# Three changes to the last stretch of an attention-and-involution kernel: own buffers for VectorE's products, weight copies made at once, additions queued by when their products should be ready

## The chip, the core and the metric

The kernel runs on one core of one Trainium2 chip. The metric is the device time of one execution in microseconds (us). The median of 3 runs before the change is 2592.14 us (2591.94 to 2592.26).

A core has several engines that run their own instruction queues in order: TensorE (PE in the profile; its weight loads are PEld), VectorE (DVE), ScalarE (ACT), GpSimd (POOL) and SyncE (SP), which here issues nearly all transfers. They meet by semaphores.

## The reference, cut to what matters

All data is float32. The input is 4 images of 512 channels and 64 x 64 pixels. Two layers follow each other.

```python
# layer 0: attention over all 4096 pixels of an image, with a residual
q = wq @ xf + bq;  k = wk @ xf + bk;  v = wv @ xf + bv        # 128 channels each
attn = softmax(q^T k)                                        # 4096 x 4096 per image
x = wo @ (v @ attn^T) + bo + x                               # back to 512 channels

# layer 1: involution, a 7x7 filter whose weights depend on the pixel
out = relu(s1 * (W1 @ x) + b1)                               # 128 channels, 8 groups of 16
w = Ws @ relu(sr * (Wr @ out) + br) + bs                     # 49 taps x 8 groups per pixel
out[g, c, pixel] = sum over 49 taps of w[g, tap, pixel] * out[g, c, pixel + tap]
x = s3 * (W3 @ out) + b3 + x
```

## The kernel before, in words

For each image `b` the function `keys_values` computes keys and values, and `attention` walks over blocks of queries: score matmuls (`pss`), an exponential on ACT (`pt`), and a matmul with the values (`po`). A finished block goes to `finish_block`, a generator that divides by the sums, adds the residual, computes the first product of layer 1 (`p1`), writes its pixels to DRAM (`pix`) and makes `red`, from which the tap weights come. The last image's last block is cut into two of 256 pixels, named `7_0` and `7_256` below.

The involution is done in units. A unit is 4 rows of 64 pixels, so 16 units to an image; `b, u` names it. Pixels lie on the partitions and channels along a row. The function `weights` makes the tap weights of a unit with two matmuls into a PSUM tile `pw`. Image rows come from `pix` by DMA into `ring`, a buffer of 12 rows. The taps of a unit are grouped into instructions: one product (line 417) multiplies ring rows by tap weights, for one column offset and 1 to 4 row offsets at once, 256, 512, 768 or 1024 columns. The first products of a unit go straight into its accumulator `acc`. Every other product goes into a buffer `prod` and is then added.

While attention runs, DVE makes all products and POOL adds them (line 445). After the last `attention` call the list `tail` is filled, and only then does this stretch differ, which is the part that the change touches:

- `share` (line 185) chooses for each product who makes it and who adds it: DVE then PE, DVE then POOL, or POOL then PE. It keeps in `spent` the time that it expects each engine to have spent, and takes the choice that keeps the longest of them shortest. The prices are the constants of line 77.
- [...] when POOL first makes a product of a unit, `copied` (line 310) has ACT copy the two halves of `pw` into an SBUF tile `w`, which is taken from the pool of the x tiles.
- All products, whoever makes them, take turns in the 4 buffers of the pool `prods`.
- When PE adds, `turned_add` (line 253) issues one 128 x 128 transposing matmul for each 128 columns, accumulating in a PSUM tile `pa`. These are queued at once behind each product. A unit's `acc` is added last, by `add_sums` in `turn_unit`. The finished `pa` is copied to `accT`, and `close_chunk` multiplies it (`py`), adds the result to x and writes x out.

The loop over `finishing`, `closing` and `taps` at the end of `fast_path` issues one step of each in turn. A recording layer then orders the instructions on each engine; in the last stretch it may move products. Two engines that read the same PSUM tile are made to wait for each other by that layer, in the order in which the code names them.

In the last stretch three units are left, 13, 14 and 15 of image 3, besides the end of unit 12 on POOL and the end of block `7_256`.

Of the kernel before, what the change touches and what calls it, by code (L numbers as in the profile page):

```python
# [15 lines left out]
P = 128  # L16
CT = C // P
CH = 512
# [55 lines left out]
HOP_US = 0.8  # L74
STEP_US = 1.0
POOL_LAG = 4.0, 7.5
DVE_COL, POOL_COL, PE_ADD = (0.064, 1.042e-3), (0.13, 2.19e-3), 0.115
PIECE = 3
TB = 32
WARM = 8  # L80
# [7 lines left out]
def fast_path(  # L88
# [22 lines left out]
    def pool(name, bufs, **kw):  # L111
        return ctx.enter_context(tc.tile_pool(name=name, bufs=bufs, **kw))

    const = pool("const", 1)
    xpool = pool("x", 6)
    kvpool = pool("kv", 1)
    ptpool = pool("pt", 5)
    redpool = pool("red", 3)
    work1 = pool("work1", 1)
    work2 = pool("work2", 2)  # L120
    prods = pool("prods", 4)
    scratch = pool("scratch", 1, space=bass.MemoryType.DRAM)
    ps = pool("ps", 2, space=bass.MemoryType.PSUM)
    ps1 = pool("ps1", 1, space=bass.MemoryType.PSUM)
# [2 lines left out]
    ps_s = scorepool.enter_context(  # L127
        tc.tile_pool(name="ps_s", bufs=2, space=bass.MemoryType.PSUM, reuse_waits="tile")
    )
    wpools, early = [ps1], {}  # L130

    wt = const.tile([P, O_WR], F32, name="wt")
    vec = const.tile([P, NVEC], F32, name="vec")
# [29 lines left out]
    due, seen = 0.0, 0.0  # L163
    free = {"dve": 0.0, "pool": 0.0, "dma": 0.0}
    tail = []
    spent = {}
    reds, sums_c = {}, {}
    written = {}
    landing = {}
# [14 lines left out]

    def share(cols, adds, direct):

        by = {
            "dve": DVE_COL[0] + DVE_COL[1] * cols,
            "pool": POOL_COL[0] + POOL_COL[1] * cols,
            "pe": PE_ADD * cols / P,  # L190
        }
        ways = [("dve", "pe"), ("dve", "pool"), ("pool", "pe")]
        if direct:
            ways = ways[:1]

        def after(way):
            us = dict(spent)
            us[way[0]] += by[way[0]]
            if adds:
                us[way[1]] += by[way[1]]  # L200
            return us

        way = min(ways, key=lambda w: sorted(after(w).values(), reverse=True))
        spent.update(after(way))
        return way
# [102 lines left out]


    def copied(b, u, pw):  # L310
        w = xpool.tile([P, CT, CH], F32, tag="x", name=f"w_{b}_{u}")
        for t in range(NT):
            nc.scalar.copy(w[:, t, : NTAP * G], pw[:, t, : NTAP * G])
        return w

    def weights(b, u):
# [31 lines left out]
    def involution():  # L348
        nonlocal low, due
        while True:  # L350
            while not units:
                yield "none"
            b, u = units.pop(0)
            acc = work2.tile([P, NT, 4, P], F32, tag="acc", name=f"acc_{b}_{u}")
            yield from until(free["dve"] + 0.3)
            pw = early.pop((b, u), None) or weights(b, u)
            begin = pe + 0.5
            pw_copy = None
            pa, ops = None, []
            base = b * STEP + u * UR  # L360
            for dy0, n in DYS:

                at = (base + dy0) % RING
                whole = at + n + NT < RING + 1
                pieces = [(dy0, n)] if whole else [(dy0, 2), (dy0 + 2, n - 2)]
                ops += [((0, 1), x, dy, k) for x in range(K) for dy, k in pieces]
            ending = (b, u) == (B - 1, NU - 1)
            if ending:

                ops = [op for op in ops if op[2] < DYS[1][0]]  # L370
                for x in range(K):
                    ops += [((0, 1), x, 4, 1), ((0,), x, 5, 2)]
            for o, (tiles, x, dy, n) in enumerate(ops):
                if o and dy >= DYS[1][0] > ops[o - 1][2]:
                    low = base + UR
                    pump()
                    if tail and units:
                        early[units[0]] = weights(*units[0])
                rows = [(base + dy + t * 2) % RING for t in range(NT)]
                while base + dy + n + 2 * tiles[-1] > load:  # L380
                    yield "wait"
                landed = max(landing[base + dy + 2 * t + i] for t in tiles for i in range(n))
                while not tail and (
                    pe < max(begin, landed)
                    or free["dve"] > pe + (4.5 if b == B - 1 else 3.5)
                    or free["pool"] > pe + lag
                ):
                    yield "wait"
                first = x == 0 and dy < DYS[1][0]
                maker = adder = None  # L390
                if tail:
                    maker, adder = share(
                        n * len(tiles) * P, not first, first or ending and o >= len(ops) - 6
                    )
                cost = n * len(tiles) / NT
                free["pool"] = max(free["pool"], takes("dve", DVE_TAPS[0] + DVE_TAPS[1] * cost))
                takes("pool", POOL_TAPS[0] + POOL_TAPS[1] * cost)
                due -= cost
                d0 = dy - DYS[dy >= DYS[1][0]][0]
                prod, p0 = acc, d0  # L400
                if not first:
                    prod, p0 = prods.tile(
                        [P, NT, 4, P], F32, tag="prod", name=f"prod_{b}_{u}_{o}"
                    ), 0
                nt = len(tiles)
                col = (x * K + dy) * G
                lines = ring[:, rows[0] : rows[0] + n, x, :]
                image = bass.AP(
                    tensor=lines.tensor, offset=lines.offset,
                    ap=[lines.ap[0], [(rows[1] - rows[0]) * K * P, nt], [K * P, n], [1, P]],  # L410
                )
                maps = pw
                if maker == "pool":
                    if pw_copy is None:
                        pw_copy = copied(b, u, pw)
                    maps = pw_copy
                product = (nc.gpsimd if maker == "pool" else nc.vector).tensor_tensor(  # L417
                    prod[:, :nt, p0 : p0 + n, :].rearrange("p t d (g c) -> p t d g c", g=G),
                    image.rearrange("p t d (g c) -> p t d g c", g=G),
                    maps[:, :nt, col : col + n * G].unsqueeze(3)  # L420
                    .broadcast_to([P, nt, n * G, GC])
                    .rearrange("p t (d g) c -> p t d g c", d=n),
                    ALU.mult,
                )
                if not tail:
                    tc.keep_in_program_order(product)
                if first:
                    pass
                elif adder == "pe":

                    begun = pa is not None
                    if not begun:
                        pa = ps1.tile([P, NT, P], F32, tag=("po", "acc")[u % 2], name=f"pa_{b}_{u}")
                    closes = ending and o == len(ops) - 1
                    if closes:
                        add_sums(pa, acc, False)
                    for t in tiles:
                        for d in range(n):
                            turned_add(
                                pa[:, t, :], prod[:, t, d, :],  # L440
                                not begun and t == d == 0,
                                closes and t == tiles[-1] and d == n - 1,
                            )
                else:
                    nc.gpsimd.tensor_tensor(  # L445
                        acc[:, :nt, d0 : d0 + n, :], acc[:, :nt, d0 : d0 + n, :],
                        prod[:, :nt, :n, :], ALU.add,
                    )
                yield
            low = max(low, (b + 1) * STEP if u == NU - 1 else base + UR)  # L450
            pump()
            if pa is None:
                for n in (2, 1):
                    nc.gpsimd.tensor_tensor(  # L454
                        acc[:, :, :n, :], acc[:, :, :n, :], acc[:, :, n : 2 * n, :], ALU.add
                    )
            closing.append(turn_unit(b, u, acc, pa, takes("pool", POOL_OP * 1.5)))


    def add_sums(pa, acc, closes):  # L460
        for t in range(NT):
            for d in range(4):
                spend("pe", PE_ADD)
                turned_add(
                    pa[:, t, :], acc[:, t, d, :], False, closes and t == NT - 1 and d == 3
                )


    def turn_unit(b, u, acc, pa, done):
        c, k = divmod(u, 2)  # L470
        yield from until(done + 2.0)
        for _ in range(7 if tail else 0):
            yield
        if pa is None and b < B - 1:

            blocks = work2.tile([P, NT * P], F32, tag="turned", name=f"turned_{b}_{u}")
# [316 lines left out]
    for b in range(B):  # L793
# [26 lines left out]
            )  # L820
        attention(b, *kv)
    tail.append(True)
    spent.update(pe=0.0, **{e: max(free[e] - pe, 0.0) for e in ("dve", "pool")})
    scorepool.close()
    wpools.insert(0, pool("ps_w", 1, space=bass.MemoryType.PSUM, reuse_waits="tile"))
# [405 lines left out]
```

## Time and profile before

| | before |
|---|---|
| median of 3 runs | 2592.14 us |
| the profiled execution's own time | 2591.92 us |
| its span | 2590.0 us |
| granted TensorE clock, mean | 0.999 |
| last `po` matmul ends, from the start of the span | about 2532.1 us |
| first `pa` add of the last stretch | 2536.24 us |
| last `x<-py` on DVE starts (two in 0.92 us) | 2584.14 us |

A span is the time from the first to the last instruction. In a row of the timeline the first number is the start in us, the second the length, then engine, line, operation, tiles (`out<-in`), shapes and how many instructions the row merges; in brackets stands the idle time before it and what ended it. A row of the waits names who waited for whom, the total in us, how often, and the longest. A wait for several semaphores is put down to the one that came last. A 512-column float32 matmul shows as two records, a transposing add as one.

### The profile page before, as it was taken

To read this page: it belongs to the slowest core of one execution; us is meant where nothing else is said; L and a number is where in the kernel's file an instruction comes from. 1 tells how busy PE (TensorE), PEld (TensorE's weight loads), DVE (VectorE), ACT (ScalarE), POOL (GpSimd) and SP (SyncE) were. 2 spreads that over 40 slices of the span, in tenths; PEclk is the share of its full clock that TensorE was granted. 3 is DMA by queue.
4 is the path that set the end of the run, shared out by engine and by line. 5 is a ranking of instruction groups with operands and counts; after the bars stand their busy time and mean duration, and the time that the engine had idled before them with its cause. 6 is when DMAs were issued, how large, how long until landed. Compare 5 with 4: busy or idle time off the path is not lost.

```text
span 2590.0 us, 24394 instructions
## 1 busy us (share of the span) xinstructions
PE 2575.1 (99%) x7398; PEld 1232.7 (48%) x7398; DVE 1861.7 (72%) x2668; ACT 838.0 (32%) x1385; POOL 1814.8 (70%) x1198
## 2 busy tenths in 40 slices
PE   9999999999999999999999999999999999999998
PEld 7444444445544444444554444444464444444476
DVE  0347778887585787888666667887856678787887
ACT  1333333332233333333223333333323333333331
POOL 0006788877881778888786368887878477787985
PEclk9999999999999999999999999999999999999999
DMA  6033233445615343234651434434363431332343
GB/s 238 1 74 63 57 78 82 98 101 150 153 54 114 63 101 76 65 82 93 169 149 41 108 69 98 100 69 102 79 182 101 116 94 48 79 77 61 77 108 88
DMA packets 208473, 243.36 MB, mean 94 GB/s; under 512 B 109576, under 2 KB 128464, under 8 KB 208208
## 3 DMA queue, kind: packets, MB, share of 16 engines
q1 hardware_dynamic: 207904, 241.39, 38.6%
q8 instruction: 59, 0.97, 0.2%
q14 instruction: 78, 0.64, 0.1%
q10 hardware_dynamic: 432, 0.36, 0.1%
HBM read 192.65 MB, written 49.06 MB: 93 GB/s over the span
## 4 chain that ended last, share of the span: by engine, by line
PE 91%; POOL 4%; DVE 3%; issue 1%; DVEq 0%; POOLq 0%; ACT 0%; ACTq 0%
PE pss L251 32%; PE po L251 31%; PE pv L251 4%; PE pk L251 4%; PE pq L251 4%; PE py L251 4%; PE pwo L251 4%; PE p L251 4%; POOL acc L445 3%; PE pw L251 2%; DVE prod L417 1%; DVE pacc L783 1%; PE pa L255 1%; PE pr L251 1%; POOL acc L454 0%
## 5 line engine op out<-in xcount | busy, mean ns | idle before, releaser
L445 POOL TENSOR_TENSOR acc<-acc,prod 128x768 f32<-128x768 f32 (+3 forms) x1044 | 1670.7, 1618 | 740.2 <-DVE prod L417 696.8
L251 PE MATMUL pss<-q,k 128*128 128x512 f32 (+1 forms) x2112 | 1055.7, 584 | 0.0
L251 PE MATMUL po<-pt,v 128*128 128x512 f32 (+1 forms) x2112 | 1047.2, 580 | 0.0
L752 ACT ACTIVATE pt<-pss 128x512 f32<-128x512 f32 x1024 | 611.0, 597 | 1242.7 <-PE pss L251 1171.4
L417 DVE TENSOR_TENSOR prod<-ring,pw 128x768 f32<-128x768 f32 (+3 forms) x1081 | 875.3, 844 | 51.2 <-POOL acc L445 45.0
L783 DVE TENSOR_TENSOR pacc<-pacc,pt 128x512 f32<-128x512 f32 x958 | 665.5, 695 | 237.5 <-ACT pt L752 209.4
L251 PEld LDWEIGHTS po<-pt,v 128*128 128x128 f32 x2112 | 398.8, 190 | 480.9 <-issue 460.4
L251 PEld LDWEIGHTS pss<-q,k 128*128 128x128 f32 x2112 | 391.5, 190 | 466.8 <-issue 462.0
L478 DVE STREAM_TRANSPOSE turned<-acc 128x256 f32<-128x256 f32 x48 | 21.4, 445 | 217.8 <-POOL acc L454 217.8
L251 PE MATMUL py<-accT,wt 128*128 128x512 f32 (+1 forms) x264 | 132.3, 584 | 4.1 <-DVE x L534 3.3
L251 PE MATMUL pwo<-on,wt 128*128 128x512 f32 (+1 forms) x264 | 128.5, 579 | 0.0
L454 POOL TENSOR_TENSOR acc<-acc 128x512 f32<-128x512 f32 x122 | 121.4, 995 | 9.6
L251 PEld LDWEIGHTS pv<-wt,x 128*128 128x128 f32 x1024 | 119.6, 192 | 15.3 <-issue 15.3
L534 DVE SCALAR_TENSOR_TENSOR x<-py,vec,x 128x512 f32<-128x512 f32 (+1 forms) x132 | 95.8, 727 | 36.9 <-PE py L251 36.7
L251 PE MATMUL pv<-wt,x 128*128 128x128 f32 x1024 | 120.2, 275 | 0.0
L251 PE MATMUL p<-x,wt 128*128 128x512 f32 (+1 forms) x264 | 119.3, 580 | 0.0
L251 PE MATMUL pk<-x,wt 128*128 128x512 f32 x256 | 117.5, 598 | 0.0
L663 ACT ACTIVATE x<-x,vec 128x512 f32<-128x512 f32 (+1 forms) x132 | 93.0, 707 | 72.3 <-PE p L251 58.2
L251 PE MATMUL pq<-x,wt 128*128 128x512 f32 (+1 forms) x264 | 115.3, 579 | 0.0
L636 DVE SCALAR_TENSOR_TENSOR x<-pwo,bo,x 128x512 f32<-128x512 f32 (+1 forms) x132 | 95.3, 728 | 21.8 <-PE pwo L251 20.4
L417 DVE TENSOR_TENSOR acc<-ring,pw 128x1024 f32<-128x1024 f32 (+1 forms) x84 | 78.7, 956 | 16.4 <-PE pw L251 15.6
L251 PEld LDWEIGHTS pq<-x,wt 128*128 128x128 f32 x264 | 50.1, 190 | 59.7 <-issue 56.4
(71 smaller groups left out, 731.4 us busy)
## 6 DMA issues: line engine op xcount, KB each, us to landing
x<-x_dram SPq DMA_DIRECT2D x55, 1024.0 KB, 5.7
ring<-pix SPq DMA_DIRECT2D x74, 448.0 KB, 6.7
ring<-pix SPq DMA_DIRECT2D x24, 1344.0 KB, 9.7
out_dram<-x SPq DMA_DIRECT2D x31, 1024.0 KB, 4.5
ring<-pix SPq DMA_DIRECT2D x24, 896.0 KB, 10.6
ring<-pix SPq DMA_DIRECT2D x30, 672.0 KB, 10.8
ring<-pix SPq DMA_DIRECT2D x6, 2240.0 KB, 19.5
pix<-o1t SPq DMA_DIRECT2D x192, 32.0 KB, 1.7
```

Source lines behind the costliest of these rows:

```text
L251: return nc.tensor.matmul(o, lhsT=lhsT, rhs=rhs, start=start, stop=stop)
L255: nc.tensor.matmul(o, lhsT=lhsT, rhs=ident, start=start, stop=stop, is_transpose=True)
L417: product = (nc.gpsimd if maker == "pool" else nc.vector).tensor_tensor(prod[:, :nt, p0 : p0 + n, :].rearrange("p t d (g c) -> p t d g c", ...
L445: nc.gpsimd.tensor_tensor(acc[:, :nt, d0 : d0 + n, :], acc[:, :nt, d0 : d0 + n, :], prod[:, :nt, :n, :], ALU.add,)
L454: nc.gpsimd.tensor_tensor(acc[:, :, :n, :], acc[:, :, :n, :], acc[:, :, n : 2 * n, :], ALU.add)
L478: nc.vector.transpose(blocks.rearrange("p (t k q) -> p t k q", t=NT, q=TB), acc[:, :, 0, :].rearrange("p t (k q) -> p t k q", q=TB),)
L534: nc.vector.scalar_tensor_tensor(xt[:, t, :], py, v1(V_S3 + t), xt[:, t, :], ALU.mult, ALU.add)
L636: nc.vector.scalar_tensor_tensor(xt[:, t, :], pw, bo[:, t : t + 1], xt[:, t, :], ALU.add, ALU.add)
L663: nc.scalar.activation(xt[:, t, :], xt[:, t, :], AF.Identity, bias=v1(V_B3 + t))
L752: nc.scalar.activation(pt, pss, AF.Exp)
L783: nc.vector.tensor_tensor(paccs[k], paccs[k], pt, ALU.add)
```

## The change

Nothing is changed before the last stretch but the place of pools in SBUF.

- The pool of keys and values gets a stack of its own, opened after the others, and is closed when the last attention is issued. Two new pools take its room: `tail_w`, 3 tiles for weight copies, and `tail`, 5 buffers for the products that DVE makes. POOL's products stay in the 4 buffers of `prods`.
- The copy of a unit's weights is issued when its first product is, or, for the next unit, right behind its `weights`, whether POOL turns out to need it or not.
- POOL's price for a product is told apart from that for an addition.
- PE's additions are not queued at once. They go into a list with the time at which the maker should be done; `drain` queues, in order of these times, all that lie behind the time DVE has reached by the plan, and the rest of a unit when the unit is closed.

The diff, cut to its core:

```diff
-DVE_COL, POOL_COL, PE_ADD = (0.064, 1.042e-3), (0.13, 2.19e-3), 0.115
+DVE_COL, POOL_COL, POOL_ADD, PE_ADD = (0.064, 1.042e-3), (0.19, 1.66e-3), (0.13, 2.19e-3), 0.115
...
-    kvpool = pool("kv", 1)
...
     prods = pool("prods", 4)
+    kvstack = ExitStack()
+    kvpool = kvstack.enter_context(tc.tile_pool(name="kv", bufs=1, reuse_waits="tile"))
+    tailpools = []
...
     def share(cols, adds, direct):
-        by = {
+        made = {
             "dve": DVE_COL[0] + DVE_COL[1] * cols,
             "pool": POOL_COL[0] + POOL_COL[1] * cols,
-            "pe": PE_ADD * cols / P,
         }
+        added = {"pool": POOL_ADD[0] + POOL_ADD[1] * cols, "pe": PE_ADD * cols / P}
...
     def copied(b, u, pw):
-        w = xpool.tile([P, CT, CH], F32, tag="x", name=f"w_{b}_{u}")
+        w = tailpools[0].tile([P, NT, NTAP * G], F32, tag="w", name=f"w_{b}_{u}")
...
                     if tail and units:
                         early[units[0]] = weights(*units[0])
+                        copies[units[0]] = copied(*units[0], early[units[0]])
...
                 if tail:
+                    if pw_copy is None:
+                        pw_copy = copies.pop((b, u), None) or copied(b, u, pw)
                     maker, adder = share(
...
                 if not first:
-                    prod, p0 = prods.tile(
+                    home = tailpools[1] if maker == "dve" else prods
+                    prod, p0 = home.tile(
...
                 elif adder == "pe":
-                    begun = pa is not None
...
-                    for t in tiles:
-                        for d in range(n):
-                            turned_add(
...
+                    closes = ending and o == len(ops) - 1
                     if closes:
-                        add_sums(pa, acc, False)
...
+                        drain(sums)
+                        add_sums(sums["pa"], acc, False)
+                    adds.append((spent[maker], o + 100 * u, sums, prod, tiles, n, closes))
...
+                if tail:
+                    drain()
                 yield
...
+    def drain(unit=None):
+        due = sorted(a for a in adds if a[2] is unit or a[0] <= spent["dve"] or a[6])
+        for a in due:
+            adds.remove(a)
+            _, _, sums, prod, tiles, n, closes = a
...
+            for t in tiles:
+                for d in range(n):
+                    turned_add(
+                        sums["pa"][:, t, :], prod[:, t, d, :],
...
     def turn_unit(b, u, acc, sums, done):
...
         for _ in range(7 if tail else 0):
             yield
+        drain(sums)
+        pa = sums.get("pa")
...
     tail.append(True)
+    kvstack.close()
+    tailpools += [pool("tail_w", 3, reuse_waits="tile"), pool("tail", 5, reuse_waits="tile")]
```

## The prediction

> **What bounds the kernel now.** I read the page first: engine totals, then the chain that ended last.
>
> ```profile
> PE 2575.1 (99%) x7398; PEld 1232.7 (48%) x7398; DVE 1861.7 (72%) x2668; ACT 838.0 (32%) x1385; POOL 1814.8 (70%) x1198
> ...
> PE 91%; POOL 4%; DVE 3%; issue 1%; DVEq 0%; POOLq 0%; ACT 0%; ACTq 0%
> ```
>
> TensorE is busy throughout and carries the chain. The orders of the two built programs are the same on all five queues until the attention of the last image ends (last `po` at 2532.1 us), so I keep that time. What can move is the 57.9 us behind it, where units 13, 14 and 15 of image 3 are made. I read this by stretches, then the engines' timelines, then the waits.
>
> ```profile
> 2532.90:2545.00 12.10, 11.49 (x78) 9.11 (x77) 10.59 (x19) 4.01 (x9) 6.90 (x6) 1.00 0.41 125
> 2545.00:2550.80 5.80, 5.43 (x46) 4.72 (x44) 5.09 (x10) 0.96 (x3) 3.07 (x5) 1.00 1.05 211
> ...
> 2556.70:2568.00 11.30, 9.68 (x60) 6.54 (x58) 10.13 (x12) 0.87 (x2) 7.59 (x6) 1.00 0.11 44
> ...
> 2575.00:2582.00 7.00, 6.14 (x39) 4.47 (x37) 4.40 (x12) 0.67 (x2) 1.58 (x3) 1.00 0.23 77
> ```
>
> The columns are length, then busy time (and instructions) of PE, PEld, DVE, ACT, POOL, then granted clock (1.00, so no throttling). PE looks full even here, but a `pa` record (0.272 us) is longer than its pace, so short waits hide in it:
>
> ```profile
> 2536.24 0.49 PE L255 MATMUL pa<-ident,prod 128*128 128x128 f32 x3
> ...
> 2542.57 2.13 PE L255 MATMUL pa<-ident,prod 128*128 128x128 f32 x18
> ...
> 2545.90 4.67 PE L255 MATMUL pa<-ident,prod 128*128 128x128 f32 x36
> ...
> 2581.22 0.38 PE L255 MATMUL pa<-ident,prod 128*128 128x128 f32 x2
> 2582.12 2.41 PE L251 MATMUL py<-accT,wt 128*128 128x256 f32 x8 [0.52 <-ACT accT L517]
> ```
>
> Eighteen adds in 2.13 us is (2.13 - 0.272)/17 = 0.109 each; 56 in 6.33 us elsewhere gives 0.110; the 36 in 4.67 us take 0.126, so 0.6 us there is hidden waiting. I use 0.110. From the first `pa` (2536.24) to the end of the last (2581.60) are 45.4 us. PE's own work in it: 270 adds x 0.110 = 29.7; four 512-column `py` x 0.865 (0.86 to 0.87 in the chain) = 3.5; four 256-column `py` and four `pwo` x 0.44 (the chain has two `pwo` in 0.89) = 3.5; `pw_15` 0.9; `pn` 0.1; the last `p`, `pp` and `pr` 1.1. Sum 38.8, so PE waits **6.6 us**. From the end of the last `pa` to the end of the span are 8.4 us, which the change does not touch. The waits say for what:
>
> ```profile
> ACT w L313 <- DVE acc L417: 10.7, 2, 7.0
> POOL prod L417 <- PE pa L255: 7.0, 11, 1.5
> ...
> POOL prod L417 <- ACT w L313: 4.7, 2, 4.2
> DVE prod L417 <- PE pa L255: 4.5, 8, 0.9
> POOL acc L445 <- DVE prod L417: 3.9, 3, 2.7
> ```
>
> It is a ring: both makers wait for one of four shared buffers, which PE frees; PE waits for a product of the slower maker; POOL waits for a weight copy that itself stands behind a DVE product.
>
> **The change, part by part.**
>
> *Room.* The DVE's product pool and the pool of weight copies now lie where keys and values lay. Their last readers are the last `pss` (2528.6) and `po` (2532.1), before any tail product in either order: 0. The other pools shift in address. No row shows a cost of an address; the runs' spread bounds it to 0.3 us either way, I take 0.
>
> *Buffers.* DVE gets five of its own, POOL keeps the four. In the new order most DVE products wait only for PE's adds of five DVE products ago. This is what ends DVE's 4.5 us and most of POOL's 7.0.
>
> *Weight copies.* Six ACT copies (0.49 each, 0.88 a pair) move ahead; they issue no DMA, and the wait for an x buffer's old output transfer goes. `pw_13` ends at 2532.9, so `w_13` is ready at 2533.9 instead of 2541.6, and POOL starts unit 13 when its unit 12 ends (2537.5): its 4.18 us of idle time go. `w_14`'s second half now stands behind `o1t` and `red` on ACT, done near 2538; POOL wants it near 2546.8. `w_15` cannot come before `pw_15`, which PE reaches behind `py_6_0_2`, near 2558; ready at 2559.9, about 2 us after POOL is free. That wait stays.
>
> In the new order the DVE's first product of each unit waits for these copies. Before, the row `ACT w <- DVE acc` shows the reverse, ACT waiting for DVE. The Trainium skill (PSUM — Partial Sum Buffer, section on bank collisions) says two engines may not touch one bank and quadrant at once, two readers included, and that nothing in hardware stalls them, so software must. By that rule each pair locks DVE out for 0.88: 3 x 0.88 = 2.6 us against this change, and a sum of 2588.9. By the rows the copies end 0.8 us (unit 13), 9 us (14) and 1.5 us (15) before DVE reaches them, because other DVE work stands ahead. I take 0 and keep 2.6 for the range.
>
> *The start.* DVE's `rls`, `spread` and `on` now stand before `acc_13` instead of between products. The reduction ends at 2532.95 and `pl` at 2533.62; then 0.20 + 0.45 + 0.40 less overlap puts `acc_13` at 2534.7 (before 2532.97), and `prod_13_1`, after 1.14 + 1.20, at 2537.0. DVE idles 0.7 us before `rls`, and PE's first add is **0.8 late**. In exchange the last `p`, `pp`, `pr` are done before it: **-1.1** from PE's queue behind. `o1t` is 1.9 earlier; SP's order is unchanged, so its two `pix` and first two `ring` transfers go out 1.9 earlier. The DMA rows show the four ring loads (2.24 MB in all) at some 210 GB/s, ending near 2553.7 before, so near 2552 now. DVE wants the last one at 2552.7, and PE its product only at 2559.7: covered; 1 us later would still be.
>
> *Who makes what.* The new prices move work to POOL: two products of 512 more, one of 256 less, one addition of 768 more: +2 x 1.06 - 0.62 + 1.82 = +3.3, from 24.3 to 27.6 us. DVE loses 2 x 0.60 and gains 0.33. PE loses six adds: **-0.7**. From their starts, without waits: POOL 2537.6 + 27.6 = 2565.2; DVE near 2570.6; PE 2537.0 + 37.0 = 2574.0 (264 adds 29.0, the rest 8.0). PE is still the longest.
>
> *Order of adds.* Sorted by the time at which the products should be ready, they are queued so that PE rarely meets an unfinished one. Walking the new order with the durations above, margins (product ready / PE there) are: 13_6 2543.1/2543.4, 13_20 2547.8/2549, 14_12 2553.1/2556.4, 15_1 2561.9/2563, 15_2 2563.7/2563.9, 15_3 2564.9/2564.9. POOL's unit 15 runs from 2559.9: 1.93 + 1.82 + 1.93 + 1.93 + 0.62 + 0.73 = 2568.9, second addition 2569.6. DVE's 15_11 and 15_12 wait for these buffers, and `x<-py_7_0_0` stands behind 15_12 to 15_17 (near 2571.5). `py_7_0_2` needs its bank and waits about **1.2**. This is the new wait. With 0.5 for thin margins PE waits **1.7** instead of 6.6.
>
> **The sum.** +0.8 - 1.1 - 0.7 - 4.9 = -5.9 on the profiled execution (2591.92, span 2590.0): span about 2584.2. The profiled execution lies 0.2 below the median of 2592.14; I apply -5.8 to the median: **2586.3**. The unknown is PE's remaining wait: none at all would give 2584.6, all 6.6 kept 2591.2.
>
> **The rivals.** *Likeliest*: as above, 2585.4 to 2586.9. For it: every margin comes from durations that hardly vary in the tail (1.93 for each 1024-column POOL product). Chance 0.72.
>
> *POOL decides unit 15.* It starts 2 us late for lack of `w_15`, DVE then waits for its additions, and every microsecond of POOL passes to the end. Two more lost there, or the DVE locked out for the 2.6 us above, give 2588.3 to 2588.9. Against it: POOL has 5 us of idle time earlier. Chance 0.20.
>
> *The change does not act*: the makers' rates, not buffers, cause PE's waits; all 6.6 stay, 2591.2. Against it: the sums above leave PE longest by over 3 us. Chance 0.04.
>
> *Slower*: POOL keeps its idle pattern and carries 3.3 us more. Before, it had 40.0 us from 2537.5 to its last addition (2577.5) for 24.3 of work, so 15.7 idle. With 27.6 of work and the same idle time it ends at 2580.8, and the closing adds behind it 3.3 later: 2595.4. It decides from 12.4 us of idle time on; my walk has about 5.5. For it: POOL's four buffers are still freed by PE alone, and 13_14 and 13_16 wait some 3 us for that. Chance 0.04.
>
> **How the numbers follow.** 2586.3 is the likeliest case. The range runs from 2585.4 (waits near 0.8) to 2588.4 (the nearer POOL case); some 3 in 100 lie below and 14 above. 0.2% is 5.2 us, a border at 2587.0, about what a measurement of this kernel can tell from no change: faster 0.72, same 0.24 (POOL decides, or no effect), slower 0.04. The forecast lies only 0.6 beyond the border.
>
> **What would show it.** Right: `w_13` near 2533 and POOL's first product near 2537.6; first `pa` near 2537.0 (later than before); the wait of DVE products for `pa` near 0, POOL's near 3; `pa` runs at 0.110 from 2540 to 2570; one PE wait of about 1 us before `py_7_0_2`; last `pa` ending near 2575.7, span 2584.2. Wrong: PE gaps between the adds of units 14 or 15 with POOL as releaser; POOL idle over 8 us behind 2537; DVE idle before `acc_13`, `acc_14` or `acc_15` with ACT as releaser; a change before 2532.

## The result

The changed kernel takes 2588.39 us (median of 22 runs, 2587.34 to 2590.11) against 2592.68 us before (22 runs, 2591.94 to 2595.68): 4.3 us less, ratio 0.9983 with a 95% interval of [0.9977, 0.9990]. The forecast was 2586.3 us, 5.8 less than the 2592.14 of its own three runs. The profiled execution took 2587.85 us, its span 2586.1 (before: 2591.92 and 2590.0).

The page of the changed kernel, engine totals and the chain that ended last:

```profile
PE 2572.9 (99%) x7392; PEld 1232.5 (48%) x7392; DVE 1860.2 (72%) x2667; ACT 838.4 (32%) x1385; POOL 1818.6 (70%) x1200
...
PE 88%; POOL 5%; DVE 4%; issue 2%; ACT 0%; POOLq 0%; DVEq 0%; ACTq 0%
```

PE has six instructions fewer, POOL 3.8 us more work. The stretches of the last part (columns as in the prediction's view):

```profile
2532.90:2545.00 12.10, 12.02 (x78) 9.38 (x77) 11.10 (x20) 4.84 (x11) 8.61 (x9) 1.00 0.46 136
2545.00:2550.80 5.80, 5.80 (x55) 5.80 (x55) 5.80 (x12) 0.37 (x1) 4.32 (x6) 1.00 1.02 214
...
2556.70:2568.00 11.30, 11.30 (x82) 8.90 (x82) 11.05 (x15) 0.87 (x2) 9.72 (x6) 1.00 0.25 93
...
2575.00:2582.00 7.00, 4.20 (x26) 2.97 (x24) 2.34 (x6) 0.37 (x1) 0.00 (x0) 1.00 0.40 133
```

From 2545.00 to 2550.80 TensorE now does 55 matmuls where it did 46, and from 2556.70 to 2568.00 it does 82 where it did 60. POOL has nothing left after 2575. The waits of the same stretch (waiting engine and tile, releaser, us in total, times, longest):

```profile
ACT w L315 <- PE pw L253: 6.5, 3, 5.7
POOL prod L419 <- PE pn L345: 3.3, 1, 3.3
...
POOL prod L419 <- issue: 1.6, 1, 1.6
...
POOL prod L419 <- PE pa L257: 1.4, 1, 1.4
DVE prod L419 <- DMA ring<-pix: 1.2, 1, 1.2
PE py L253 <- DVE x L552: 1.0, 1, 1.0
```

The ring of waits is open: copies wait for `pw` and no longer for a DVE product; DVE products no longer wait for `pa`; POOL's wait for `pa` fell from 7.0 us in 11 pieces to 1.4 in one, with 3.3 more that the view puts down to `pn`. (That wait stands before POOL's fifth product, with its four buffers full, and `pn` is the TensorE matmul right behind the adds that end at 2544.7, so it is most likely a wait for a buffer too.) TensorE's adds run at full pace, and one wait of 1.0 us is left, the one before `py_7_0_2`:

```profile
2561.15 8.03 PE L257 MATMUL pa<-ident,prod 128*128 128x128 f32 x72
...
2573.40 0.70 PE L253 MATMUL py<-accT,wt 128*128 128x256 f32 x2 [0.96 <-DVE x L552]
...
2576.55 0.38 PE L257 MATMUL pa<-ident,prod 128*128 128x128 f32 x2
2577.45 2.41 PE L253 MATMUL py<-accT,wt 128*128 128x256 f32 x8 [0.52 <-ACT accT L535]
```

72 adds in 8.03 us is (8.03 - 0.27)/71 = 0.109 each. What the forecast had not got is at the beginning of the stretch. TensorE from the last `po` on, in the changed kernel:

```profile
2532.09 0.93 PE L253 MATMUL pw<-wt,red 33*128 33x392 f32 x4
2533.10 0.61 PE L253 MATMUL pl<-blocks,quads 128*128 128x8 f32 x4
2533.64 0.92 PE L253 MATMUL pw<-wt,red 33*128 33x392 f32 x2
2534.49 1.99 PE L253 MATMUL p<-x,wt 128*128 128x256 f32 x8
2536.32 0.59 PE L253 MATMUL p<-on,w1wo 128*128 128x256 f32 x2
2536.85 0.92 PE L253 MATMUL pw<-wt,red 33*128 33x392 f32 x2
2537.70 0.44 PE L693 MATMUL pp<-ident,o 128*128 128x128 f32 x2
2538.07 0.44 PE L253 MATMUL pr<-o,wt 128*64 128x128 f32 x4
2538.44 0.66 PE L257 MATMUL pa<-ident,prod 128*128 128x128 f32 x4
```

and in the kernel before:

```profile
2533.55 0.93 PE L251 MATMUL pw<-wt,red 33*128 33x392 f32 x4
2534.41 1.99 PE L251 MATMUL p<-x,wt 128*128 128x256 f32 x8
```

The first `pa` is at 2538.44, 2.2 us later than before and 1.4 later than forecast, and no row ahead of it from `pl` on has an idle time: TensorE is not waiting there, it works. `pw_14` stands twice in that queue. A pair of `pw` matmuls (each passes as two records) lies in two halves of the array's rows (partitions from 0 and from 64 on in the code) and runs as one: 4 records from 2533.55 until the next matmul at 2534.41, 0.86. In the new order the two halves of `pw_14` are apart, the five `p` between them, and each half takes by itself what the pair took: 2533.64 to 2534.49 and 2536.85 to 2537.70, 0.85 each. `pw_13` at 2532.09, in the same trace, is a whole pair in 0.93. The Trainium skill (TensorE: Matmul & The Clock Gate, Part 3: Packing small matmuls) says that matmuls in different row groups run concurrently and that TensorE takes matmuls strictly in their order; the rows agree: one that has no partner next to it in the queue has nothing to run beside. Why the recording layer parts the two halves here is not known.

### The profile page after: what moved, and what is told of

Its sections match the earlier page's. It is cut to its first block, busy times and chain, and to the rows that moved or that the text cites. A ratio compares the mean times of both kernels' runs of the same rounds, so it can differ in the third digit from the quotient of the medians.

```text
span 2586.1 us, 24367 instructions
## 1 busy us (share of the span) xinstructions
PE 2572.9 (99%) x7392; PEld 1232.5 (48%) x7392; DVE 1860.2 (72%) x2667; ACT 838.4 (32%) x1385; POOL 1818.6 (70%) x1200
## 4 chain that ended last, share of the span: by engine, by line
PE 88%; POOL 5%; DVE 4%; issue 2%; ACT 0%; POOLq 0%; DVEq 0%; ACTq 0%
PE pss L253 31%; PE po L253 30%; POOL acc L439 5%; PE pv L253 4%; PE pk L253 4%; PE pq L253 4%; PE p L253 4%; PE pwo L253 4%; PE py L253 4%; PE pw L253 2%; DVE prod L419 2%; DVE pacc L801 1%; PE pa L257 1%; PE pr L253 1%; POOL acc L450 0%
```

## The experiments

Executions of one kernel differ by 2 to 4 us, and so do the profiles, by what happens ahead of the changed stretch (the last `po` ends between 2531.8 and 2534.2 us), so kernels are compared by what follows the last `po`: the start of the first `pa` and the end of the last one, counted from the end of that `po`. Before: +4.18 and +49.54. Changed: +6.28 and +44.78. In the table below "first `ok`" is the length of the first comparison `ok<-rls` on DVE, and "adds" counts TensorE's transposing adds; a ratio is taken against the runs of the kernel before in the same rounds.

| kernel | first `pa` | last `pa` ends | first `ok` | adds | time, us | ratio to before |
|---|---|---|---|---|---|---|
| before | 4.18 | 49.54 | 0.16 | 270 | 2592.68 | 1 |
| changed | 6.28 | 44.78 | 1.09 | 264 | 2588.39 | 0.9983 [0.9977, 0.9990] |
| e1_stt | 6.28 | 44.76 | 1.09 | 264 | 2587.45 | 0.9981 [0.9975, 0.9988] |
| e2_two | 6.28 | 44.77 | 1.08 | 264 | 2587.72 | 0.9982 [0.9974, 0.9989] |
| e9_tt | 6.28 | 44.76 | 1.10 | 264 | 2587.64 | 0.9980 [0.9973, 0.9987] |
| e11_program | 6.28 | 44.77 | 0.17 | 264 | 2588.02 | 0.9983 [0.9975, 0.9991] |
| e10_tt_early | 6.28 | 43.51 | 1.08 | 264 | 2586.98 | 0.9979 [0.9971, 0.9987] |
| e12_prog_early | 6.28 | 43.51 | 0.17 | 264 | 2586.90 | 0.9977 [0.9968, 0.9986] |
| e7_before_bufs | 4.17 | 48.15 | 0.16 | 270 | 2591.93 | 0.9995 [0.9987, 1.0004] |
| e7_before_copies | 6.28 | 51.28 | 1.08 | 270 | 2594.01 | 1.0006 [0.9998, 1.0015] |
| e7_before_both | 6.28 | 45.27 | 1.09 | 270 | 2588.31 | 0.9984 [0.9977, 0.9990] |
| e3_shared | 6.28 | 49.79 | 1.08 | 264 | 2592.72 | 1.0001 [0.9993, 1.0010] |
| e4_late | 4.17 | 48.42 | 0.16 | 264 | 2591.78 | 0.9997 [0.9988, 1.0005] |
| e6_price | 6.28 | 44.78 | 1.08 | 270 | 2587.92 | 0.9983 [0.9976, 0.9989] |

### What made the start late: a first theory, and how it fell

The first thing that I saw in the two traces was not the split pair. It was DVE's small comparison `ok<-rls`, 32 columns, which took 0.16 us before and 1.09 now, ahead of `on` and `acc_13`. DVE and POOL in the changed kernel:

```profile
2533.99 0.46 DVE L641 STREAM_TRANSPOSE spread<-rls 128x256 f32<-128x256 f32 x1
2534.36 1.09 DVE L336 TENSOR_SCALAR ok<-rls 128x32 f32<-128x32 f32 x1
2535.37 0.41 DVE L645 TENSOR_TENSOR on<-on,spread 128x256 f32<-128x256 f32 x1
...
2529.82 5.59 POOL L439 TENSOR_TENSOR acc<-acc,prod 128x768 f32<-128x768 f32 x3
2535.49 2.08 POOL L450 TENSOR_TENSOR acc<-acc 128x512 f32<-128x512 f32 x2
```

It ends at 2535.45; POOL's running addition ends at 2529.82 + 5.59 = 2535.41. One microsecond on DVE, and one microsecond missing from the result: I took the one for the cause of the other. The first two experiments try the comparison in another form, and twice.

**e1_stt.**

```diff
-        nc.vector.tensor_scalar(o, rl, SAFE[0], None, ALU.is_ge)
+        if cols.stop is None:
+            nc.vector.scalar_tensor_tensor(
+                o, rl, SAFE[0], ones[:, : B * N // TB - EARLY], ALU.is_ge, ALU.mult
+            )
+        else:
+            nc.vector.tensor_scalar(o, rl, SAFE[0], None, ALU.is_ge)
```

> The changed kernel, with one VectorE instruction in another form: the last comparison ok<-rls (128x32, SBUF to SBUF, 1.09 us long in the changed kernel, 0.16 before) is made as a scalar_tensor_tensor with a second input of ones; same values. Theory (held by POOL): a tensor_scalar between SBUF tiles can't run while POOL's addition runs (2533.61 to 2535.41), which the other form can. Then the instruction takes about 0.2 us, on<-on,spread starts near 2534.5 instead of 2535.37, the first pa near 2537.6 instead of 2538.44, the last pa ends near 2576.0 instead of 2576.93, and the span is some 0.9 us shorter, near 2585.2. Rival (its own neighbours): it waits because it reads rls straight behind reciprocal and spread on the same engine; then the new form takes about 1 us too and nothing moves (span 2586.1). Third outcome: a form with two SBUF inputs is held by POOL as well; then also about 1 us.

Measured: 1.09 us again, again until POOL's addition ends; first and last `pa` as in the changed kernel. The form does not matter, or not this one. The median, 2587.45, is 0.9 below that of the changed kernel, just what the theory had forecast, yet the tail is the same to 0.02 us: the medians alone would have misled.

**e2_two.**

```diff
         nc.vector.tensor_scalar(o, rl, SAFE[0], None, ALU.is_ge)
+        if cols.stop is None:
+            nc.vector.tensor_scalar(o, rl, SAFE[0], None, ALU.is_ge)
```

> The changed kernel with that comparison issued twice in a row (the same result written again). Theory (held by POOL): the first ends with POOL's addition near 2535.4; the second either slips into the gap before POOL's next instruction (0.1 us more) or is held until that ends (a fold of 1.28 us, so near 2536.7): 0.1 or 1.3 us more, and each long one ends with a POOL instruction. Last pa end near 2577.0 or near 2577.9, since PE then starts its adds later still. Rival (its own neighbours): the second finds the wait already over: 0.1 us; or a fixed cost of 1.09 each, ending nowhere near a POOL end.

Measured: the first took 1.08. The second did not follow it, but was ordered 8 us later, where POOL has nothing to do:

```profile
2536.24 1.08 DVE L336 TENSOR_SCALAR ok<-rls 128x32 f32<-128x32 f32 x1
...
2544.80 0.17 DVE L338 TENSOR_SCALAR ok<-rls 128x32 f32<-128x32 f32 x1
...
2539.39 4.12 POOL L421 TENSOR_TENSOR prod<-ring,w 128x1024 f32<-128x1024 f32 x4
```

POOL's four products end at 2543.51. The same operation on the same data: 1.08 beside a running POOL operation, 0.17 beside an idle POOL. What two of them right behind each other would do, this run does not show.

**e9_tt.** Three `tensor_tensor` against constants in the place of the two comparisons.

```diff
+            nc.vector.tensor_tensor(o, rl, safe[:, 0, :], ALU.is_ge)
+            nc.vector.tensor_tensor(rl, rl, safe[:, 1, :], ALU.is_le)
+            nc.vector.tensor_tensor(o, rl, o, ALU.mult)
```

> The changed kernel with the two comparisons of the last check rewritten as tensor_tensor operations against a constant tile (three small operations instead of two, same values). Theory (VectorE's small comparison waits until GpSimd's running addition ends, 1.09 us instead of 0.16; tensor_tensor is not held, as the 212 to 371 additions of 128x512 show, 0.69 to 0.70 us whether GpSimd runs or not): the first comparison takes 0.15 to 0.25 us beside a running GpSimd operation, on starts 2.4 to 2.6 us behind the end of the last po (after: 3.2), the first pa 5.4 to 5.6 behind it (after: 6.28), the last pa 43.8 to 44.0 behind it (after: 44.78), time about 0.9 us below the changed kernel: 2587.5. Rival 1 (the operation is slow because it reads what the operation just ahead wrote, whoever runs beside it): again about 1.1 us, and nothing is gained. Rival 2 (every operation of VectorE with all operands in SBUF is held while GpSimd runs): the first or a later one of the three takes over 0.9 us, first pa at 6.2 or later. Rival 3 (the 1.0 us is given back later because another engine decides the end): first pa at 5.5, last pa still near 44.8.

Measured: 1.10. Rival 2 fits; on this run alone rival 1, an operation that reads what the one ahead has just written, fits too. Against rival 1 speaks that the long comparison ends 0.04 to 0.05 us behind POOL's operation in every trace that has it, that `spread`, which reads `rls` right behind its making, keeps its length (0.46, before 0.45), and a case in e7_before_copies below. The expectation leaned on the additions `pacc`, 0.69 to 0.70 us whether POOL runs or not, and that was misread: `pacc` is a PSUM tile (it comes from `ps1`), so only one of its operands lies in SBUF. The Trainium skill has the rule (SBUF — State Buffer, Who interferes with whom): DVE and GpSimd share one pair of SBUF ports as an exclusive lock; a DVE instruction with two SBUF inputs contends with a GpSimd instruction that reads SBUF, a `tensor_scalar` can enter a mode that takes the pair, and the one that comes second is blocked for the whole of the other instruction. The rows agree in all forms: 1.08 to 1.10 for `tensor_scalar`, `scalar_tensor_tensor` and `tensor_tensor` with all operands in SBUF, while `on<-on,spread`, whose `spread` is in PSUM, takes 0.41 beside POOL's next operation (before: 0.40). Nearly all the rest of DVE's tail is operations with an operand in PSUM.

**e11_program.** So the operation can't be made cheap by its form; it can be put elsewhere.

```diff
-        nc.vector.tensor_scalar(o, rl, SAFE[0], None, ALU.is_ge)
+        first = nc.vector.tensor_scalar(o, rl, SAFE[0], None, ALU.is_ge)
+        if cols.stop is None:
+            tc.keep_in_program_order(first)
```

> The changed kernel, with the first comparison of the last check kept at its place in the program, behind the last pwo additions to x, where GpSimd is idle; nothing else is touched. Theory (a VectorE operation whose operands all lie in SBUF, two of them read or a tensor_scalar, is held until the running GpSimd operation ends; operations with an operand in PSUM are not): on starts 2.3 to 2.5 us behind the end of the last po (after: 3.21), the first pa 5.3 to 5.5 behind it (after: 6.28), both comparisons take 0.16 to 0.3 us; last pa 43.8 to 44.1 us behind the end of the last po (after: 44.78), time about 0.8 us below the changed kernel, 2587.5. Rival 1 (whatever stands at this place is slow, for instance the operation behind spread): on itself is held, the first pa again near 6.2. Rival 2 (the microsecond at the start was hidden, since GpSimd decides when unit 15 comes): the first pa at 5.4, but the last pa still within 0.2 us of 44.8 and TensorE's wait before py_7_0_2 about 1.9 us instead of 0.96.

```profile
2534.34 0.42 DVE L647 TENSOR_TENSOR on<-on,spread 128x256 f32<-128x256 f32 x1
2534.68 1.21 DVE L421 TENSOR_TENSOR acc<-ring,pw 128x1024 f32<-128x1024 f32 x1
...
2542.14 0.17 DVE L336 TENSOR_SCALAR ok<-rls 128x32 f32<-128x32 f32 x1
```

On DVE it did what was expected: the comparison takes 0.17, `on` starts 2.40 us behind the last `po` (3.21 in the changed kernel). On TensorE it did nothing:

```profile
2536.11 0.59 PE L253 MATMUL p<-on,w1wo 128*128 128x256 f32 x2
2536.64 0.92 PE L253 MATMUL pw<-wt,red 33*128 33x392 f32 x2
2537.49 0.44 PE L695 MATMUL pp<-ident,o 128*128 128x128 f32 x2
2537.86 0.44 PE L253 MATMUL pr<-o,wt 128*64 128x128 f32 x4
2538.23 0.66 PE L257 MATMUL pa<-ident,prod 128*128 128x128 f32 x4
```

First `pa` +6.28, last +44.77, to a hundredth as in the changed kernel. The theory and rival 2 had the first `pa` a microsecond earlier; rival 1 had it near 6.2, but because `on` would be held, and `on` took 0.42. The theory falls: the hold is real and costs DVE a microsecond, but TensorE's own queue up to the first `pa` is 6.28 us long, and the held product was ready at +5.87 (`prod_13_1` ends at 2538.03). What is left is TensorE's queue, where the split pair stands. All ten other kernels of the table with prompt copies have it and have the first `pa` at +6.28, whatever DVE does; the three with late copies have the pair whole and the first `pa` at +4.17 or +4.18, ahead of `p<-on`:

```profile
2533.70 0.93 PE L253 MATMUL pw<-wt,red 33*128 33x392 f32 x4
2534.56 1.99 PE L253 MATMUL p<-x,wt 128*128 128x256 f32 x8
2536.39 0.49 PE L257 MATMUL pa<-ident,prod 128*128 128x128 f32 x3
```

(e4_late, TensorE.) The arithmetic closes: from +4.17 on, the changed kernel has the last `p` (0.52 until the next instruction), half of `pw_14` (0.85), `pp` (0.37) and `pr` (0.37), and 4.17 + 2.11 = 6.28. A version of the changed kernel with only the pair kept together was not tried; that it would win the whole 0.85 is not shown, since the held product would then be late by some 0.4 us (5.87 against 6.28 - 0.85 = 5.43). So the split's cost is read from the rows, not from a kernel without it.

### What brought the gain

**e7_before_bufs, e7_before_copies, e7_before_both**: the kernel before, with one part or both (e7_before_both is the two edits together). Only the core of each edit is shown; the room for the new pools is made as in the change.

```diff
 # buffers
-                    prod, p0 = prods.tile(
+                    home = tailpools[1] if maker == "dve" else prods
+                    prod, p0 = home.tile(
 # copies
-        w = xpool.tile([P, CT, CH], F32, tag="x", name=f"w_{b}_{u}")
+        w = tailpools[0].tile([P, NT, NTAP * G], F32, tag="w", name=f"w_{b}_{u}")
...
                         early[units[0]] = weights(*units[0])
+                        copies[units[0]] = copied(*units[0], early[units[0]])
...
+                    if pw_copy is None:
+                        pw_copy = copies.pop((b, u), None) or copied(b, u, pw)
```

> The kernel before, with the room of keys and values given to five buffers of DVE's products alone; copies, prices and the order of adds as before. Theory (both waits must go): DVE's waits for pa (4.5 us before) go, but POOL still starts unit 13 near 2541.7, behind its weight copy, and PE waits for POOL's products at the starts of units 14 and 15 (0.8 and 1.6 us) and about 1 us before py_7_0_2: last pa ends near 2580.1 against 2581.6, a gain of 1.4 us, near 2591.2 in time. Rival (buffers are the cause): most of the gain of the whole change, 3 us or more. Rival (copies are the cause): no gain.

> The kernel before, with the weight copies in their own three tiles and issued at once; all products still share four buffers, prices and order of adds as before. Theory (both waits must go): POOL's first product needs a buffer that PE frees only behind DVE's products, so POOL starts near 2541.9 although its copy is ready at 2533.9; the last pa ends within 0.5 us of before (2581.6), and the late start of DVE and the comparison held by POOL are paid as in the changed kernel: no gain, 2592.2 to 2592.8. Rival (copies are the cause): POOL starts near 2537.6 and 3 us or more are gained.

> The kernel before with its own buffers for VectorE's products and with the prompt copies, but with the old price of GpSimd's product, and the additions still queued by the old key. Tells what the two buffer parts do together, and so what is left for the price and the order. Theory (the two waits must go together: alone the buffers brought 1.4 us and the copies cost 1.7): together they bring 4.0 to 4.6 of the 4.77 us on the tail, last pa 45.0 to 45.6 us behind the end of the last po (before: 49.55, after: 44.78), TensorE with 270 additions. Rival (price and order carry it): last pa at 47 or later. The first pa about 6.3 us behind the last po, as in the changed kernel, since the first comparison again falls beside GpSimd's addition.

Measured, on the end of the last `pa`: buffers alone -1.39, copies alone +1.74, both -4.27. Buffers alone and both came as expected; copies alone lost more than the 0.5 us forecast (2594.01 against 2592.2 to 2592.8). Neither is a gain of its own that the runs' times can tell from none; together they are nearly the whole change. e7_before_copies carries the split pair, and in it a second comparison was held too, for 1.35 us, until POOL's product ended at 2544.26:

```profile
2542.96 1.35 DVE L337 SCALAR_TENSOR_TENSOR ok<-rls,ok 128x32 f32<-128x32 f32 x1
...
2542.32 1.94 POOL L420 TENSOR_TENSOR prod<-ring,w 128x1024 f32<-128x1024 f32 x1 [4.72 <-DVE prod L420]
```

In the changed kernel the same comparison, also behind an `x<-pwo,bo,x`, takes 0.18 with POOL idle. So it is POOL's operation that counts, and not the neighbour on DVE.

**e3_shared** takes the own buffers out of the changed kernel, **e4_late** the prompt copies.

```diff
 # e3_shared
-                    home = tailpools[1] if maker == "dve" else prods
+                    home = prods
 # e4_late
-                        copies[units[0]] = copied(*units[0], early[units[0]])
...
+                if maker == "pool" and pw_copy is None:
+                    pw_copy = copied(b, u, pw)
```

> The changed kernel with VectorE's products back in the pool of four that GpSimd's products share; prompt copies, price and order stay. Theory: VectorE waits again for pa to free the shared buffers, and TensorE gets back 4 to 5 us of idle: last pa 48.3 to 49.3 us behind the end of the last po (after: 44.78), time about 4 us above the changed kernel: 2592 to 2593. Rival (with copies, price and order in place the buffers no longer matter, since GpSimd no longer holds one for long): last pa within 0.5 us of 44.8, time unchanged.

> The changed kernel with the copies of the weights made when GpSimd's first product is reached, as before the change; own buffers, price and order stay. Theory (buffers and copies must go together): GpSimd starts late and idles, last pa 47.8 to 49.0 us behind the end of the last po (after: 44.78; before with the buffers alone: 48.15), first pa about 4.2 behind it, since VectorE's order is that of before and the first comparison falls where GpSimd is idle (0.16 us). Rival (the order of additions alone removes the waits, and the copies only move the start): last pa 45.5 or earlier.

Measured: +5.01 and +3.64. Without its own buffers the changed kernel ends later than the kernel before (49.79 against 49.54). e3_shared went 0.5 beyond its expectation, e4_late came as expected, the comparison at 0.16 with POOL idle included. Each of the two waits stands behind the other. With the copies late (e4_late) POOL's first product comes at +8.70 from the last `po` instead of +5.37, and TensorE waits 2.1 us for POOL's products. With the buffers shared POOL starts late as well, although `w_13` is ready: at +8.38 in e3_shared, where it waits for TensorE to free a buffer, and at +10.12 in e7_before_copies (the wait of 4.72 above):

```profile
2540.55 1.94 POOL L419 TENSOR_TENSOR prod<-ring,w 128x1024 f32<-128x1024 f32 x1 [2.97 <-PE pa L257]
```

(e3_shared, POOL.)

**e6_price** puts the old price of a POOL product back.

```diff
-DVE_COL, POOL_COL, POOL_ADD, PE_ADD = (0.064, 1.042e-3), (0.19, 1.66e-3), (0.13, 2.19e-3), 0.115
+DVE_COL, POOL_COL, POOL_ADD, PE_ADD = (0.064, 1.042e-3), (0.13, 2.19e-3), (0.13, 2.19e-3), 0.115
```

> The changed kernel with the old fixed price of a GpSimd product (0.13 instead of 0.19), so that GpSimd gets the work shares of before. Tells what the new price brings. Theory (six additions fewer on TensorE, 0.7 us, against GpSimd's load): TensorE runs 270 additions again, last pa 45.0 to 45.5 us behind the end of the last po (after: 44.78), of it 0.7 us of additions less what TensorE waits for at the end. Rival (the price does nothing for the end, which GpSimd sets): last pa within 0.1 us of 44.8.

Measured: 270 adds again, and the last `pa` still at +44.78; TensorE's wait before `py_7_0_2` is gone, and one of 0.40 before an add at +12.1 is all that is left. The rival's number holds (that POOL sets the end does not follow, since TensorE hardly waits here): the six adds that the price takes from TensorE, 0.65 us, come back as 0.56 of waiting. From e7_before_both (45.27) to e6_price (44.78) only the order of the adds is new: 0.49 us. So of the 4.76 us on the tail the buffers and the copies together make 4.27, the order 0.49 and the price nothing.

### A version that ends earlier

**e10_tt_early and e12_prog_early** issue the next unit's weights and copy from a unit's sixth product on (on top of e9_tt and e11_program).

```diff
-                    if tail and units:
-                        early[units[0]] = weights(*units[0])
-                        copies[units[0]] = copied(*units[0], early[units[0]])
+                if tail and units and units[0] not in early and o >= 6:
+                    early[units[0]] = weights(*units[0])
+                    copies[units[0]] = copied(*units[0], early[units[0]])
```

> As e9_tt, and in the last stretch each unit's weights and their copy are issued from the sixth product of the unit before on, instead of at its second half. Theory: w of unit 15 is then there before GpSimd wants it (its idle 1.6 us before prod_15_1 goes), and TensorE's wait of 1.0 us before py_7_0_2 goes with it: the last pa 42.6 to 43.1 us behind the end of the last po, 1.7 to 2.2 us less than in the changed kernel, time 2586.0 to 2586.7. Rival (GpSimd's idle only moves, to where it waits for pa to free its buffers): the wait before py_7_0_2 stays 0.7 us or more, last pa near 43.8 as in e9_tt. Rival (weights issued early make TensorE or ScalarE wait for the bank that pw needs): a wait of PE on ACT or POOL of over 0.5 us in the first units, last pa later than 43.9.

> As e11_program, with each unit's weights and their copy issued from the sixth product of the unit before on. That early issue took 1.27 us off the tail (44.78 to 43.51) with the comparison still held. Theory: the two add up: first pa 5.3 to 5.5 us behind the end of the last po, last pa 42.4 to 42.8 behind it, TensorE without a wait from the first pa on; time 2.0 to 2.3 us below the changed kernel, 2585.6 to 2586.5. Rival (with the start earlier GpSimd is the bound): a wait of TensorE of 0.5 us or more before py_7_0_2, last pa 43.0 or later.

Measured: +43.51 in both, 1.27 less than the changed kernel, and TensorE without any wait from the first `pa` to the last. Of e12's tail, only `accT` is waited for, behind the last `pa`:

```profile
PE py L253 <- ACT accT L537: 0.5, 1, 0.5
```

`pw_15` moved from +27.2 to +20.2, `w_15` is there in time, and POOL's last addition ends 1.57 us earlier. Both expectations (42.6 to 43.1 and 42.4 to 42.8) are missed by about what the held comparison was thought to be worth, and e12 got no more than e10: the comparison was off the path. The times, 2586.98 and 2586.90, are the lowest of all; their intervals overlap with that of the changed kernel, and what tells them apart is the tail. From the first `pa` to the end of the last are 37.2 us, and the prediction's sum of TensorE's own work there is 37.0: that work is nearly the whole of it now.

## Why the prediction was right, and where its size was off

- **The number**: 2588.39 is inside the range of 2585.4 to 2588.4 by 0.01 us, which is luck where executions differ by 2 to 4 us and the median before was itself 0.54 higher than the 2592.14 the forecast started from. Taken as a difference it is less close: 4.3 us less, where the range ended at 3.7 less. The likeliest case (up to 2586.9, chance 0.72) did not come, and a gain of 0.2% is not shown: it is 0.17%, with an interval of 0.10 to 0.23%.
- **The mechanism**: right. Five signs came as written: `w_13`'s copies at 2533.1 to 2533.9, POOL's first product at 2537.53 (2537.6), no DVE product waiting for `pa`, adds at 0.109 between 2540 and 2570, and one wait of 0.96 before `py_7_0_2` (1.2). POOL waited 3.3 + 1.4 = 4.7 for its buffers instead of 3, if the wait put down to `pn` is one of these, and idled 7.5 us in all up to its last addition (5.5 forecast; 8 was the sign of being wrong). The first `pa`, the end of the last one (2576.93 for 2575.7) and the span came late.
- **"PE's first add is 0.8 late ... in exchange -1.1"**: this step failed. It set the first add by the time its product is ready and credited the work done before it, but did not check how long TensorE's own queue is at that point. By the rows it is 4.17 + 0.52 + 0.37 + 0.37 = 5.43 us long without the split, longer than the 4.9 forecast, and the split, which the step did not count, adds 0.85. The start came 2.10 late (from the last `po`), so the two terms are +2.1 - 1.1 = +1.0 and not -0.3. Work moved ahead of the first add is no gain where TensorE has no idle time to put it in: 1.26 of the 2.10 is that work, which the -1.1 gives back, and the rest is the split. The `rls` and `spread` of the step are right (0.21, 0.46); `ok`, which it does not name, took 1.09, and made no difference.
- **"PE loses six adds: -0.7"**: the adds went, but e6_price shows that the end does not move by it.
- **Waits, 6.6 to 1.7**: by the same count 44.78 - 6.28 - 37.0 = 1.5, so -5.1 instead of -4.9.
- **The sum**: +2.1 - 1.1 - 0.7 - 5.1 = -4.8; the tail shortened by 49.54 - 44.78 = 4.76. The forecast was -5.9. The start is 1.3 worse and the waits 0.2 better than forecast, which is the missing 1.1 us.
- **"8.4 us from the end of the last `pa` to the end of the span, which the change does not touch"**: 9.1 in this profile, 8.4 to 9.4 in all of them, without order by kernel. The last `py` and x rows keep their distances; the difference lies after the last output transfer's issue. In these two profiles it takes 0.7 off the gain in the span (some 4.0 us in all), and no kernel of the table moves it.
- **Weight copies against DVE, 0 or 2.6**: 0, as chosen; no wait of DVE for a copy is in the view. That holds with the copies early; in e4_late, where they are late, DVE waits 1.9 us for them (waits of its tail):

```profile
DVE prod L418 <- ACT w L315: 1.9, 2, 1.0
```

- **Ring loads "covered"**: right. DVE waited 1.2 us for one (the row `DVE prod <- DMA ring<-pix`), and TensorE did not.
- **The rivals**: POOL deciding unit 15 did not come, though the time fell near that case, for another reason. POOL idled 1.6 us until `w_15` was there (the row `POOL prod <- issue`; 2 forecast), and removing that in e10 and e12 was worth 1.3 us. POOL did not keep its idle pattern.

## What to carry to other kernels

When work is moved ahead of an instruction, add up the queue of the engine that executes it, not only the readiness of its data: the later of the two counts. Matmuls that are to run side by side must stay neighbours in TensorE's queue, and a scheduler may part them. A delay of the right size in the right place is still no cause: take it away and look whether the bound engine moves, and where two waits form a ring, try them together, since each alone may gain nothing.

## What the runs showed of the hardware

- Half of a pair of 33-row matmuls with 392 columns costs TensorE as much as the pair: 0.85 us for one, 0.86 for two side by side.
- A DVE operation of 32 columns with all its operands in SBUF took 1.08 to 1.35 us instead of 0.16 to 0.19 when it met a running POOL operation, ending 0.04 to 0.05 us behind it, in three instruction forms.
